# Reordering the small work around the projections of an adaLN Mamba2 block with a binarized feed-forward layer

## The chip, the cores and the metric

The kernel runs on one core of one Trainium2 chip. The metric is the device time of one execution in microseconds (us). All arithmetic is fp32. The engines are called PE (matmul), PEld (weight load of PE, overlapping it), DVE (VectorE), ACT (ScalarE), POOL (GpSimd) and SP (SyncE, which issues most of the DMAs).

## The reference

Input is x of 4 sequences of 512 tokens with 512 features, and a condition c of 4 x 512. Cut to what matters:

```
mod = (silu(c) @ wmod) split into sa, ca, ga, sb, cb, gb      # one row for each sequence
ga, gb = sign(ga)*max(|ga|, 0.25), sign(gb)*max(|gb|, 0.25)
h   = layernorm(x)*(1 + ca) + sa
x   = x + ga * mamba(h)
h   = layernorm(x)*(1 + cb) + sb
x   = x + gb * (h @ bw.T + bias)

bw = stop_gradient(where(w >= 0, 1, -1)*alpha - w) + w,   alpha = mean(|w|) by row

mamba(h):
  xBC, z, A = h @ in_proj_w.T       # 2048 + 1024 + 64 columns
  x, B, C   = silu(causal conv of xBC, 4 taps)   # x: 64 heads of 16; B, C: 8 groups of 64 states
  dt        = softplus(A)
  y         = chunked scan over chunks of 128 tokens, decay exp(-cumsum(dt)) for each head
  y         = y + D * x/dt
  return (y * silu(z + z_bias)) @ out_proj_w.T
```

The binarized weight bw takes just two values in each row, alpha and -alpha. The forward value of `(bw - w) + w` is bw up to rounding.

## The kernel before, in words

The 2048 tokens are cut into eight "halves" h of T = 256 tokens, two for each sequence. A half has two chunks c of 128 tokens, and a chunk four pairs gp of the eight groups. A triple (h, c, gp) is a unit; there are 64, eight to a half. The program is a list of steps, one for each unit (the loop at L822 to L840). In each step come, in the order in which they are written,

- the listed work of this step (`steps`): the *front* of the next half, and the *tails* of chunks that are done;
- `burst` (L593): the small products gy of C with the state for this unit, and of C with B for the unit two steps on;
- `stage2` (L630 to L696): the products py of decays and x, the sum yt, the product with z (POOL, L672), and the state's update (xd on POOL L679, pst on PE L684);
- for the unit two steps on, `stage0` (loads of the running sums into decay tiles, L536 and after) and `stage1` (16 exps on ACT, L544, eight for each of two decay tiles; the mask multiply on DVE, L622). Four decay tiles, numbered 87 to 90 in the built program, are used by turns in pairs.

The front of a half (list `FRONT`, L765 on; half 1 has `SECOND`, half 0 has `FIRST`) runs under the units of the half before. It holds the layer norm; `f_hT` (PE transposes phT, L330, of which four ACT passes make hT, L347); `f_dt` (below); the projections with causal convolution of B, C and x (`conv_pair`: products at L432, an ACT pass at L445, three DVE taps at L449, a tanh and a product); turns of B and x to tokens (pt_xt, L462); and `f_z`, four tiles z_0 to z_3 (products pp_z at L432, two ACT passes uz at L511, the tanh thz at L515, a product on DVE). Before the change the list has z_0 and z_1 at step 8, z_2 at 9 and z_3 at 10; hT and f_dt of the following half come at step 3 of its own list, which is step 11 of that of z.

`f_dt` (L353 to L406) makes the step sizes: eight products pa (L366), k from 0 to 3 and both chunks, then a chain on DVE and ACT to dt, a scan on DVE, and four DMAs to memory on SP's queue: sh to sums_d (L387), es to e_d (L391), two of r to r_d (L405). They are read back, spread over partitions, by `stage0` and `f_xt`.

The tails of a chunk are `tail1` (the output projection po, L716, the residual and the second layer norm), `tail2` (four transposes ph, L735, and ACT passes to h, L737) and `tail3` (the products pf with the binarized weight, L753). They stand at the three steps after the chunk's end, with other offsets for the last three chunks (L811 to L814); tail3 of (7, 0) is called at the end of tail1 of (7, 1).

`signs` (L267 to L279) loads 128 rows of the feed-forward weight and makes sw, ±alpha: alpha by a DVE reduction (L272) and a scaling (L273), two DVE passes (L275, L276), and on POOL the subtraction and the addition of the weight (L277, L278). `turned_signs` (L281 to L286) transposes it on PE (pbw, L285) and copies it into bwT with ACT. Both are done once, for four row blocks o, in the first half's units.

What sets the order: each engine runs its queue in the order in which the scheduler put it there. The scheduler takes the program's order as priority. Three things bend it by hand. `issue_after` holds an instruction back in that order until another one is placed. `glued` (L208 to L213) places the first of a group and then the others right behind it at a raised priority. `behind` issues a piece after the last projection of its half (`H[h]["last"]`). PSUM has five banks ("mm") taken by turns for everything but gy and py, which have a bank each.

Of the kernel before, what the change touches and what calls it, by code (L numbers as in the profile page):

```python
# [2 lines left out]

# [8 lines left out]
F32 = mybir.dt.float32  # L12
AF = mybir.ActivationFunctionType
ALU = mybir.AluOpType
AX = mybir.AxisListType
PSUM = bass.MemoryType.PSUM
P = 128

B, L, DM = 4, 512, 512
# [20 lines left out]
def adaln_mamba_block(  # L40
# [164 lines left out]
        for v in (cw, cb, zb):  # L205
            nc.vector.tensor_scalar(v, v, 0.5, None, ALU.mult)

    def glued(products):  # L208

        first = products[0]()  # L210
        with tc.issue_after(first.ins), tc.high_priority(offset=1000):
            for product in products[1:]:
                product()  # L213
# [53 lines left out]
    def signs(o):  # L267

        fw = wk.tile([P, DM], F32, tag="h2", name=f"fw{o}")
        nc.sync.dma_start(fw, ffn_w[o * P : (o + 1) * P, :])  # L270
        alpha = wk.tile([P, 1], F32, tag="rs1", name=f"alpha{o}")
        nc.vector.tensor_reduce(alpha, fw, AX.X, ALU.add, apply_absolute_value=True)  # L272
        nc.vector.tensor_scalar(alpha, alpha, 1.0 / DM, None, ALU.mult)  # L273
        sw = wk.tile([P, DM], F32, tag="CB"[o % 2], name=f"sw{o}", bufs=3)
        nc.vector.tensor_scalar(sw, fw, 0.0, 2.0, ALU.is_ge, ALU.mult)  # L275
        nc.vector.tensor_scalar(sw, sw, -1.0, alpha, ALU.add, ALU.mult)  # L276
        nc.gpsimd.tensor_sub(sw, sw, fw)  # L277
        nc.gpsimd.tensor_add(sw, sw, fw)  # L278
        sws[o] = sw  # L279

    def turned_signs(h, o):  # L281
        sw = sws.pop(o)
        pt = ps.tile([P, NK, P], F32, tag="mm", name=f"pbw{o}")
        for i in range(NK):
            nc.tensor.transpose(pt[:, i, :], sw[:, i * P : (i + 1) * P], ident)  # L285
        nc.scalar.copy(bwT[:, :, o * P : (o + 1) * P], pt)  # L286


    def layer_norm(tiles, name, into=None):
# [63 lines left out]
    def f_dt(h):  # L353

        hT = H[h]["hT"]

        def small(tag, bufs=1):  # L360
            return wk.tile([P, CH], F32, tag=tag, name=f"{tag}_{h}", bufs=bufs)

        pa = ps.tile([P, CH], F32, tag="mm", name=f"pa_{h}")
        for k in range(NK):
            for c in range(2):
                mm(pa[c * NH : (c + 1) * NH, :], win[:, k, NCONV + DI :],  # L366
                   hT[:, k, KS - 1 + c * CH : KS - 1 + (c + 1) * CH], start=(k == 0), stop=(k == NK - 1))
        u, r, q, dt, relu = (small(n) for n in ("du", "dr", "dq", "da", "dl"))
        nc.vector.tensor_scalar(relu, pa, 0.0, None, ALU.max)
        nc.scalar.activation(u, pa, AF.Abs)  # L370
        nc.scalar.activation(u, u, AF.Exp, scale=-1.0)
        nc.vector.tensor_scalar(r, u, 2.0, None, ALU.add)
        nc.vector.reciprocal(r, r)
        nc.vector.tensor_mul(u, u, r)
        nc.vector.tensor_mul(q, u, u)
        nc.vector.tensor_scalar(dt, q, SERIES[0], None, ALU.mult)
        for cf in SERIES[1:]:
            nc.vector.scalar_tensor_tensor(dt, dt, cf, q, ALU.add, ALU.mult)
        nc.vector.scalar_tensor_tensor(dt, dt, 1.0, u, ALU.add, ALU.mult)
        nc.vector.scalar_tensor_tensor(dt, dt, 2.0, relu, ALU.mult, ALU.add)  # L380

        up = relu
        nc.vector.tensor_tensor_scan(up, ones, dt, 0.0, ALU.mult, ALU.add)
        sh = small("sh", 2)
        nc.vector.tensor_scalar(sh, up, up[:, CH // 2 - 1 : CH // 2], None, ALU.subtract)
        with tc.issue_after(last_win):
            nc.sync.dma_start(sums_d[h].rearrange("c h s -> (c h) s"), sh)  # L387
        es = small("es", 2)
        nc.scalar.activation(es, up, AF.Exp, scale=-1.0)
        with tc.issue_after(last_win):  # L390
            nc.sync.dma_start(e_d[h].rearrange("c h s -> (c h) s"), es)  # L391

        ntot = wk.tile([P, 1], F32, tag="ntot", name=f"ntot_{h}", bufs=1)
        nc.vector.tensor_scalar(ntot, up[:, CH - 1 : CH], -1.0, None, ALU.mult)
        ed = u
        nc.scalar.activation(ed, up, AF.Exp, bias=ntot)

        dg = q
        nc.vector.tensor_scalar(dg, ident, es[:, CH - 1 : CH], None, ALU.mult)

        nc.vector.reciprocal(r, dt)
        nc.vector.tensor_scalar(r, r, dsk, None, ALU.mult)
        with tc.issue_after(last_win):
            for c in range(2):
                nc.sync.dma_start(r_d[h, :, c, :], r[c * NH : (c + 1) * NH, :])  # L405
        H[h].update(turn=(sh, ed, dg))  # L406

    def first_dt(h):
# [21 lines left out]
    def proj(pm, h, col, lo):  # L430
        for k in range(NK):
            last = mm(pm, win[:, k, col : col + P], H[h]["hT"][:, k, lo:], start=(k == 0), stop=(k == NK - 1))  # L432
        return last.ins

    def conv_pair(h, t0, name, dst=None):

# [156 lines left out]
    def burst(old, new):  # L593

        gy = ps.tile([P, 2, 4, CH], F32, tag="gy", bufs=1, name="gy_" + "_".join(map(str, old or new)))
        products = []
        if old is not None:
            h, c, gp = old
            k = (h % HPB) * 2 + c
            if k > 0:  # L600
                products += by_rows(gy, 1, h, c, gp, states[h // HPB, k][:, gp, :])
                G[old, 1] = gy
        if new is not None:
            h, c, gp = new
            products += by_rows(gy, 0, h, c, gp, H[h]["B"][gp // 2][:, gp % 2, c * CH : (c + 1) * CH])
            G[new, 0] = gy
        glued(products)

    def stage1(h, c, gp):

# [16 lines left out]
    def stage2(h, c, gp):  # L627
# [18 lines left out]
        for r in range(2):  # L646
            glued([
                partial(
                    mm, py[32 * j : 32 * j + 32, r, :],
                    xp[:, r * 2 * P + 32 * (2 * j + q) : r * 2 * P + 32 * (2 * j + q) + 32],  # L650
                    ets[r][:, 2 * j + q, :], start=(q == 0), stop=(q == 1),
                )
                for q in range(2) for j in range(HPG // 2)
            ])

        cs = slice(c * CH, (c + 1) * CH)
        zg = H[h]["z"][gp][:, :, cs]
# [53 lines left out]
    def tail1(h, c):  # L711
        b = h // HPB
        x2 = tails[h, c]
        po = ps.tile([P, DM], F32, tag="mm", name=f"po_{h}_{c}")
        for g in range(NKI):
            last_po = mm(po, H[h]["z"][g // 2][:, g % 2, c * CH : (c + 1) * CH], wout[:, g, :],  # L716
                         start=(g == 0), stop=(g == NKI - 1))
        t = wk.tile([P, DM], F32, tag="t", name=f"t_{h}_{c}", bufs=1)
        nc.vector.tensor_mul(t, po, gates[b][:, 0, :])
        nc.vector.tensor_add(x2, x2, t)  # L720
        layer_norm([x2], f"f{h}_{c}", [t])
        nc.gpsimd.tensor_add(x2, x2, gates[b][:, 2, :])
        tails[h, c] = (x2, t)
        if (h, c) == (NHALF - 1, 1):

            with tc.issue_after(last_po.ins):
                tail3(h, 0)

# [14 lines left out]
    def tail3(h, c):  # L743
# [5 lines left out]
        for i in range(parts):  # L749
            pf = ps.tile([P, n], F32, tag="mm", name=f"pf{i}_{h}_{c}")  # L750
            cols = slice(i * n, (i + 1) * n)
            for k in range(NK):
                mm(pf, h2[:, k, :], bwT[:, k, cols], start=(k == 0), stop=(k == NK - 1))  # L753
            o = wk.tile([P, n], F32, tag="h2", name=f"o{i}_{h}_{c}")
            nc.vector.tensor_mul(o, pf, gates[b][:, 1, cols])
            nc.vector.tensor_add(o, o, x2[:, cols])
            nc.sync.dma_start(out[h * T + c * CH : h * T + (c + 1) * CH, cols], o)

    def behind(h, f, *args):
# [7 lines left out]
        (4, f_B, (0,)), (4, f_C, (0,)), (5, f_x, (0,)), (5, f_x, (1,)), (5, behind, (f_turned_sums,)), (5, behind, (f_Bt, 0)),  # L767
        (6, f_B, (1,)), (6, behind, (f_xt, 0)), (6, f_C, (1,)), (6, behind, (f_xt, 1)),
        (7, f_x, (2,)), (7, behind, (f_Bt, 1)), (7, f_x, (3,)),
        (8, f_z, (0,)), (8, behind, (f_xt, 2)), (8, f_z, (1,)), (8, behind, (f_xt, 3)),  # L770
        (9, f_z, (2,)), (10, f_z, (3,)),
    ]

    FIRST = [
# [14 lines left out]
    NU = 2 * NP  # L789
    steps = {}  # L790

    def at(step, f, *args):
        steps.setdefault(step, []).append((f, args))

    for h in range(NHALF):
        for step, f, args in (FIRST, SECOND)[h] if h < 2 else FRONT:
            at(max(0, h - 1) * NU + step, f, h, *args)
        if h % HPB == 0:
            at(h * NU + 3, load_gates, h // HPB)
        if h == 0:  # L800
# [2 lines left out]
            at(2, load_wout)  # L803
            for o in range(NK):
                at(o // 2 + 2, signs, o)
                at(o // 2 + 4, behind, 1, turned_signs, o)
    for h in range(NHALF):
        for c in range(2):
            end = h * NU + (c + 1) * NP
            at(end - 1, load_res, h, c)  # L810

            late = {(NHALF - 1, 0): (1, 3), (NHALF - 2, 1): (0, 1, 3)}.get((h, c), (0, 1, 2))
            for tail, step in zip((tail1, tail2, tail3), late):
                at(end + step, tail, h, c)  # L814

# [6 lines left out]
    for step in range(-1, max(steps) + 1):  # L822
# [9 lines left out]
        elif step < len(units):  # L832
            if new or not is_first(*units[step][:2]):
                burst(units[step], new[0] if new else None)
            stage2(*units[step])
            for unit in POST.get(step, []):
                ahead(*unit)
            for unit in new:
# [44 lines left out]
```

## Time and profile before

| what | value |
|---|---|
| runs, us | 753.33, 754.66, 755.84 (median 754.66) |
| profiled execution, us | 755.08 |
| its span, us | 753.4 |
| mean granted TensorE clock | 0.984 |
| DMA | 99.25 MB, mean 132 GB/s |
| L544 exps on ACT | 960 instructions, 293.3 us |
| L432 products of pp_x, pp_z, pp_B | 119.7, 118.1, 62.2 us |
| L716 products of po | 256 instructions, 114.2 us |

The span runs from the first to the last instruction of the profiled execution; about 1.7 us of its time lie around it. An fp32 product appears in the trace as two passes of PE, so a group of eight products counts 16. A row of the groups reads: line, engine, operation, output<-inputs, tile sizes, count, then busy time and mean ns of one, then the engine's idle time just before, with what ended most of it. In the timeline a row is a run of like instructions; the bracket is the idle time before it. A row of waits names the engine and its line, what it waited for, the total, the number of times and the longest.

### The profile page before, as it was taken

How to read it: one execution, taken by the hardware profiler on the slowest of the kernel's cores; microseconds unless marked ns; L12 is line 12 of the kernel's file. 1: busy time of each engine (PE TensorE's matmuls, PEld its weight loads, DVE VectorE, ACT ScalarE, POOL GpSimd, SP SyncE). 2: the span in 40 equal slices, each digit the busy share in tenths (PEclk: the TensorE clock that was granted, in tenths of full speed). 3: DMA queues.
4: the chain of work that ended last, by engine and by line, in shares of the span. 5: the costliest groups of instructions: out<-in, count | busy, mean ns of one | idle time of the engine just before them, and what ended most of it. 6: DMA issues, size and time to landing. Idle time of an engine off the chain costs nothing. (4 is left out here: it accounts for less than half of the span.)

```text
span 753.4 us, 15095 instructions
## 1 busy us (share of the span) xinstructions
PE 713.0 (95%) x5196; PEld 505.6 (67%) x5196; DVE 610.8 (81%) x1226; ACT 520.1 (69%) x1503; POOL 258.5 (34%) x293
## 2 busy tenths in 40 slices
PE   6999868999999999999999999999999999999977
PEld 3786646766678666767677666786666766776643
DVE  3869888876998689976999669986898849996983
ACT  2486557749696587776777596875868758798920
POOL 4022345443143322343242341353213332334540
PEclk9999979999999999999999999999999999999989
DMA  8991583636553363424563355343634337455710
GB/s 282 313 291 42 188 193 96 166 80 144 117 142 105 84 173 105 130 68 112 142 154 105 75 142 136 113 127 90 163 89 111 93 84 182 123 161 124 161 35 28
DMA packets 121308, 99.25 MB, mean 132 GB/s; under 512 B 73984, under 2 KB 99840, under 8 KB 121232
## 3 DMA queue, kind: packets, MB, share of 16 engines
q1 hardware_dynamic: 120944, 97.76, 49.8%
q8 instruction: 41, 0.67, 0.4%
q10 hardware_dynamic: 288, 0.52, 0.2%
q14 instruction: 35, 0.29, 0.1%
HBM read 92.47 MB, written 5.79 MB: 130 GB/s over the span
## 5 line engine op out<-in xcount | busy, mean ns | idle before, releaser
L544 ACT ACTIVATE decay<-decay,st 128x128 f32<-128x128 f32 x960 | 293.3, 396 | 13.5 <-DMA decay<-sums_d 13.2
L622 DVE SCALAR_TENSOR_TENSOR decay<-decay,gm 128x1024 f32<-128x1024 f32 x120 | 155.3, 1295 | 28.3 <-ACT decay L544 26.4
L432 PE MATMUL pp_x<-hT,win 128*128 128x259 f32 x512 | 119.7, 388 | 0.0
L432 PE MATMUL pp_z<-hT,win 128*128 128x256 f32 x512 | 118.1, 383 | 0.0
L716 PE MATMUL po<-wout,z 128*128 128x512 f32 x256 | 114.2, 598 | 0.0
L679 POOL TENSOR_TENSOR xd<-xpad,st 128x256 f32<-128x256 f32 x48 | 35.0, 729 | 212.5 <-PE pst L684 161.1
L432 PEld LDWEIGHTS pp_x<-hT,win 128*128 128x128 f32 x512 | 96.2, 192 | 17.3 <-issue 2.6
L432 PEld LDWEIGHTS pp_z<-hT,win 128*128 128x128 f32 x512 | 94.3, 189 | 16.1 <-issue 3.0
L669 POOL TENSOR_TENSOR yt<-yt,xs 128x256 f32<-128x256 f32 x46 | 43.7, 950 | 128.5 <-DVE yt L668 115.9
L716 PEld LDWEIGHTS po<-wout,z 128*128 128x128 f32 x256 | 47.9, 191 | 53.8 <-issue 53.2
L449 DVE SCALAR_TENSOR_TENSOR u_x<-pp_x,cw,u_x 128x256 f32<-128x256 f32 x192 | 82.7, 474 | 0.8 <-ACT u_x L445 0.3
L213 PE MATMUL py<-decay,xpad 128*32 128x128 f32 x1680 | 68.8, 280 | 0.0
L511 ACT ACTIVATE uz<-pp_z,zb 128x256 f32<-128x256 f32 x64 | 26.8, 468 | 58.3 <-PE pp_z L432 58.3
L432 PE MATMUL pp_B<-hT,win 128*128 128x259 f32 x256 | 62.2, 395 | 0.8 <-DVE u_x L449 0.7
L672 POOL TENSOR_TENSOR z<-yt,z 128x256 f32<-128x256 f32 x62 | 57.2, 922 | 11.6 <-DVE yt L671 8.2
L502 POOL TENSOR_TENSOR xs<-u_x,rr 128x512 f32<-128x512 f32 x32 | 44.1, 1378 | 46.4 <-DVE u_x L454 38.4
L753 PE MATMUL pf<-bwT,h 128*128 128x512 f32 (+1 forms) x136 | 59.3, 576 | 0.6 <-ACT h L737 0.6
L432 PE MATMUL pp_C<-hT,win 128*128 128x259 f32 x256 | 59.5, 385 | 0.0
L445 ACT ACTIVATE u_x<-pp_x,cb,cw 128x256 f32<-128x256 f32 x64 | 35.1, 559 | 33.1 <-PE pp_x L432 32.9
L210 PE MATMUL py<-decay,xpad 128*32 128x128 f32 x240 | 48.0, 282 | 8.5 <-ACT decay L544 6.8
L432 PEld LDWEIGHTS pp_B<-hT,win 128*128 128x128 f32 x256 | 48.1, 194 | 11.2 <-DVE u_x L449 1.5
L432 PEld LDWEIGHTS pp_C<-hT,win 128*128 128x128 f32 x256 | 48.4, 192 | 7.8 <-issue 0.5
(155 smaller groups left out, 1144.5 us busy)
## 6 DMA issues: line engine op xcount, KB each, us to landing
decay<-sums_d SPq DMA_DIRECT2D x120, 256.0 KB
decay<-sums_d SPq DMA_DIRECT2D x120, 128.0 KB
rr<-r_d SPq DMA_DIRECT2D x64, 128.0 KB
e<-e_d SPq DMA_DIRECT2D x96, 64.0 KB
win<-in_w_inT SPq DMA_DIRECT2D x4, 1024.0 KB
xr<-in_x SPq DMA_DIRECT2D x16, 256.0 KB
res<-o SPq DMA_DIRECT2D x15, 256.0 KB
x<-in_x SPq DMA_DIRECT2D x14, 256.0 KB
```

What stands on the lines that cost most here:

```text
L210: first = products[0]()
L213: product()
L432: last = mm(pm, win[:, k, col : col + P], H[h]["hT"][:, k, lo:], start=(k == 0), stop=(k == NK - 1))
L445: nc.scalar.activation(u[:, j, :], pm[:, KS - 1 :], AF.Identity, bias=cb[:, t : t + 1], scale=cw[:, t, KS - 1 : KS])
L449: nc.vector.scalar_tensor_tensor(u[:, j, :], pm[:, k : k + T], cw[:, t, k : k + 1], u[:, j, :], ALU.mult, ALU.add)
L502: nc.gpsimd.tensor_tensor(xs, xc, rr, ALU.mult)
L544: nc.scalar.activation(ets[r][:, i, :], ets[r][:, i, :], AF.Exp, bias=H[h]["st"][:, hd : hd + 1], scale=-1.0)
L622: nc.vector.scalar_tensor_tensor(ets[r], ets[r], 1.0, bc_mid(gm[:, r, :], HPG), ALU.min, ALU.mult)
L669: ew.tensor_add(t, t, xs)
L672: ew.tensor_mul(zg, t, zg)
L716: last_po = mm(po, H[h]["z"][g // 2][:, g % 2, c * CH : (c + 1) * CH], wout[:, g, :], start=(g == 0), stop=(g == NKI - 1))
L753: mm(pf, h2[:, k, :], bwT[:, k, cols], start=(k == 0), stop=(k == NK - 1))
```

## The change

It has eight parts.

1. `signs` makes ±0.5 with one DVE pass and multiplies by the row's sum of |w| on ACT; the two POOL passes, the scaling of alpha and the second DVE pass are gone. The factor 2/DM is applied by ACT in the copy of `turned_signs`.
2. `turned_signs` comes one step later, and last in its steps' lists.
3. `glued` takes an instruction after which the first of the group is placed. `burst` and the py products of `stage2` give the newest projection product, so that they stand behind their step's projections on PE.
4. The eight pa products of `f_dt` are glued into one piece, and k runs from 3 down to 0 for h > 0.
5. For h > 1, `f_dt` is called after `stage2` of its step (`rear`) and no longer in the step's list.
6. The four DMAs of `f_dt` are issued from GpSimd's queue for h > 0.
7. The z tiles come at steps 8, 9, 10 and 11, and the turn of x_3 at step 9.
8. The tails: tail3 of (0, 0) comes one step later. tail2 of (7, 0) is called within tail1 of (7, 1), ahead of its last two products, and tail3 of (7, 0) as before after it; the two parts of the last o take another buffer tag.

```diff
-    def glued(products):
-        first = products[0]()
+    def glued(products, after=None):
+        with tc.issue_after(after) if after else nullcontext():
+            first = products[0]()
         with tc.issue_after(first.ins), tc.high_priority(offset=1000):
...
         nc.vector.tensor_reduce(alpha, fw, AX.X, ALU.add, apply_absolute_value=True)
-        nc.vector.tensor_scalar(alpha, alpha, 1.0 / DM, None, ALU.mult)
         sw = wk.tile([P, DM], F32, tag="CB"[o % 2], name=f"sw{o}", bufs=3)
-        nc.vector.tensor_scalar(sw, fw, 0.0, 2.0, ALU.is_ge, ALU.mult)
-        nc.vector.tensor_scalar(sw, sw, -1.0, alpha, ALU.add, ALU.mult)
-        nc.gpsimd.tensor_sub(sw, sw, fw)
-        nc.gpsimd.tensor_add(sw, sw, fw)
+        nc.vector.tensor_scalar(sw, fw, 0.0, 0.5, ALU.is_ge, ALU.subtract)
+        nc.scalar.activation(sw, sw, AF.Identity, scale=alpha)
...
-        nc.scalar.copy(bwT[:, :, o * P : (o + 1) * P], pt)
+        nc.scalar.activation(bwT[:, :, o * P : (o + 1) * P], pt, AF.Copy, scale=2.0 / DM)
...
+        queue = nc.sync if h == 0 else nc.gpsimd
...
-        for k in range(NK):
-            for c in range(2):
-                mm(pa[c * NH : (c + 1) * NH, :], win[:, k, NCONV + DI :],
-                   hT[:, k, KS - 1 + c * CH : KS - 1 + (c + 1) * CH], start=(k == 0), stop=(k == NK - 1))
+        ks = range(NK) if h == 0 else range(NK - 1, -1, -1)
+        glued([
+            partial(
+                mm, pa[c * NH : (c + 1) * NH, :], win[:, k, NCONV + DI :],
+                hT[:, k, KS - 1 + c * CH : KS - 1 + (c + 1) * CH], start=(k == ks[0]), stop=(k == ks[-1]),
+            )
+            for k in ks for c in range(2)
+        ])
...
-            nc.sync.dma_start(sums_d[h].rearrange("c h s -> (c h) s"), sh)
+            queue.dma_start(sums_d[h].rearrange("c h s -> (c h) s"), sh)
...
+        newest["proj"] = last.ins
         return last.ins
...
-        glued(products)
+        glued(products, newest["proj"])
...
+        last = (h, c) == (NHALF - 1, 1)
         for g in range(NKI):
+            if last and g == NKI - 2:
+                with tc.issue_after(last_po.ins):
+                    tail2(h, 0)
...
-        (8, f_z, (0,)), (8, behind, (f_xt, 2)), (8, f_z, (1,)), (8, behind, (f_xt, 3)),
-        (9, f_z, (2,)), (10, f_z, (3,)),
+        (8, f_z, (0,)), (8, behind, (f_xt, 2)), (9, f_z, (1,)), (9, behind, (f_xt, 3)),
+        (10, f_z, (2,)), (11, f_z, (3,)),
...
+            into = rear if f is f_dt and h > 1 else steps
+            into.setdefault(max(0, h - 1) * NU + step, []).append((f, (h, *args)))
...
-                at(o // 2 + 4, behind, 1, turned_signs, o)
+    for o in range(NK):
+        at(o // 2 + 5, behind, 1, turned_signs, o)
...
-            late = {(NHALF - 1, 0): (1, 3), (NHALF - 2, 1): (0, 1, 3)}.get((h, c), (0, 1, 2))
+            late = {(0, 0): (0, 1, 3), (NHALF - 1, 0): (2,), (NHALF - 2, 1): (0, 1, 3)}.get((h, c), (0, 1, 2))
...
             stage2(*units[step])
+            for f, args in rear.get(step, []):
+                f(*args)
```

The DMAs of es and of r change their queue in the same manner as that of sh.

More of the change, by code (lines that the diff above doesn't have):

```diff
@@ L1 @@
-from contextlib import ExitStack
+from contextlib import ExitStack, nullcontext
 from functools import partial
@@ L390, in f_dt @@
         with tc.issue_after(last_win):
-            nc.sync.dma_start(e_d[h].rearrange("c h s -> (c h) s"), es)
+            queue.dma_start(e_d[h].rearrange("c h s -> (c h) s"), es)
         ntot = wk.tile([P, 1], F32, tag="ntot", name=f"ntot_{h}", bufs=1)
@@ L404, in f_dt @@
             for c in range(2):
-                nc.sync.dma_start(r_d[h, :, c, :], r[c * NH : (c + 1) * NH, :])
+                queue.dma_start(r_d[h, :, c, :], r[c * NH : (c + 1) * NH, :])
         H[h].update(turn=(sh, ed, dg))
@@ L432, in proj @@
             last = mm(pm, win[:, k, col : col + P], H[h]["hT"][:, k, lo:], start=(k == 0), stop=(k == NK - 1))
+        newest["proj"] = last.ins
         return last.ins
+    newest = {}
     def conv_pair(h, t0, name, dst=None):
@@ L653, in stage2 @@
                 for q in range(2) for j in range(HPG // 2)
-            ])
+            ], newest["proj"])
         cs = slice(c * CH, (c + 1) * CH)
@@ L723, in tail1 @@
         tails[h, c] = (x2, t)
-        if (h, c) == (NHALF - 1, 1):
+        if last:
             with tc.issue_after(last_po.ins):
@@ L753, in tail3 @@
                 mm(pf, h2[:, k, :], bwT[:, k, cols], start=(k == 0), stop=(k == NK - 1))
-            o = wk.tile([P, n], F32, tag="h2", name=f"o{i}_{h}_{c}")
+            o = wk.tile([P, n], F32, tag="h2" if parts == 1 else "th", name=f"o{i}_{h}_{c}")
             nc.vector.tensor_mul(o, pf, gates[b][:, 1, cols])
@@ L790, in adaln_mamba_block @@
     steps = {}
+    rear = {}
     def at(step, f, *args):
@@ L796, in adaln_mamba_block @@
         for step, f, args in (FIRST, SECOND)[h] if h < 2 else FRONT:
-            at(max(0, h - 1) * NU + step, f, h, *args)
+            into = rear if f is f_dt and h > 1 else steps
+            into.setdefault(max(0, h - 1) * NU + step, []).append((f, (h, *args)))
         if h % HPB == 0:
```

## The prediction

> **What bounds the kernel now.** I began with the busy times on the page, and one stretch of the middle by windows (columns: stretch and its length, then busy time and count of PE, PEld, DVE, ACT and POOL, granted clock, DMA share, GB/s).
>
> ```profile
> PE 713.0 (95%) x5196; PEld 505.6 (67%) x5196; DVE 610.8 (81%) x1226; ACT 520.1 (69%) x1503; POOL 258.5 (34%) x293
> 300.00:350.00 50.00, 49.75 (x361) 36.59 (x354) 40.75 (x80) 34.29 (x99) 21.81 (x26) 1.00 0.42 107
> ```
>
> PE is busy 713.0 of 753.4 us, and in the middle 49.75 of 50. None of its matmuls is removed, so the change can win only PE's idle time, and the half clock that follows an idle. Where that is, the waits of PE tell (total, times, longest):
>
> ```profile
> PE pbw L285 <- DVE u_C L449: 7.2, 1, 7.2
> PE py L210 <- ACT decay L544: 6.8, 6, 2.4
> ...
> PE pa L366 <- ACT hT L347: 3.8, 4, 1.2
> PE ph L735 <- DVE t L300: 3.8, 2, 3.3
> PE ph L735 <- ACT decay L544: 2.0, 1, 2.0
> ...
> PE pbw L285 <- POOL sw L278: 1.3, 1, 1.3
> ```
>
> I looked each one up in PE's timeline (start, duration, and in brackets the idle time before it with its releaser). The largest:
>
> ```profile
> 99.48 1.09 PE L285 MATMUL pbw<-ident,sw 128*128 128x128 f32 x4 [7.21 <-DVE u_C L449]
> 101.92 1.11 PE L285 MATMUL pbw<-ident,sw 128*128 128x128 f32 x4 [1.35 <-POOL sw L278]
> ```
>
> Last I read the clock by windows. It was 0.50 in 95.60:105.80, 0.51 in 126.30:129.70 and in 566.60:570.00, and 0.50 in 729.20:733.90: always after idles of PE of 7.21, 2.02, 2.38 and 3.33 us, never after those of 1.0 to 1.5. At half clock four pst passes took 0.70 us instead of 0.44 (factor 1.59), sixteen pp_x passes 5.18 against 3.72 of the like pp_z (1.39). So a stretch of 3.4 us costs 0.96 to 1.27; I take 1.2.
>
> **What the Trainium skill says.** "TensorE: Matmul & The Clock Gate", Part 1, has the clock drop to half after an idle window of about 3.4 us and return after a busy one. The stretches here are 3.4 us or multiples of it, which agrees, but idles of 2.02 and 2.38 us sufficed. The same page, Part 2, has matmuls run strictly in program order, with only weight loads pulled ahead, and ACT and DVE first in, first out; the trace agrees: PE stood 7.21 us before pbw with pp_x behind it. "DMA: Bandwidth & Descriptors", "SWDGE vs HWDGE vs iDMA", has GpSimd write its DMAs' descriptors in software, with about 1 us to the first byte against 0.6; no GpSimd DMA is in the trace of before.
>
> **The change part by part.** I wrote out the order of instructions of the built program on each engine and laid durations of the trace along it, start to start.
>
> 1. *Signs (L270 to L286).* Eight GpSimd passes (4 x 1.492 and 4 x 1.305 = 11.2 us), four alpha scalings (4 x 0.144) and the dearer half of L276 go; four ACT passes of about 0.6 us (as thz, 128x512, 0.634) come, and turned_signs moves a step later and behind the step's projections. At most this wins 7.21 + 1.35, and of the 4.97 us that PE was busy at half clock some 1.4: 10.0. What is late next: the third and fourth pp_x get the PSUM banks that pbw waited for, and these are freed by DVE's u_C taps. DVE is busy all of 96:100 and saves only about 4 us here. Walking DVE's order I get about 4 us of wait at pp_x, so the gain is **6.0** (bounds 2 and 10).
> 2. *Products behind their step's projections.* ph that stood 2.02 us at 125.60 now runs after a projection: 2.02 + 1.2 = **3.2**. The six py waits on ACT's exps (0.85, 0.81, 2.38 and three of 0.92, 6.8 together, one with a half clock) get a projection of 1.8 to 3.7 us before them: 6.8 + 1.2 = **8.0**. The cover is that projection; without it (pp_B itself waits for banks) some 2 us come back. pp_B's three waits of 0.25 go too: **0.7**.
> 3. *Tail.* The last ph waits 3.33 us for DVE's layer norm, then 4.7 us run at half clock, which cost 1.8. With tail2 of (7,0) before the last two products of po and tail3 after, this is covered: **5.1** (bounds 2 and 5.5).
> 4. *pa (f_dt).* Its three waits of 1.16 at h = 2, 4, 6 vanish as such: **3.5**. But the new order makes larger ones. In before, z_3 came at step 10; its copies were over long before hT:
>
> ```profile
> 176.38 0.83 ACT L511 ACTIVATE uz<-pp_z,zb 128x256 f32<-128x256 f32 x2
> 177.09 2.45 ACT L544 ACTIVATE decay<-decay,st 128x128 f32<-128x128 f32 x8
> 179.43 0.65 ACT L515 ACTIVATE thz<-uz 128x512 f32<-128x512 f32 x1
> 179.95 2.46 ACT L544 ACTIVATE decay<-decay,st 128x128 f32<-128x128 f32 x8
> 182.29 1.92 ACT L347 ACTIVATE hT<-phT,modT 128x256 f32<-128x256 f32 x4
> ...
> 182.91 0.44 PE L366 MATMUL pa<-hT,win 128*64 128x128 f32 x4 [1.16 <-ACT hT L347]
> ```
>
> The reader sees that ACT's queue, not the matmul, sets when pa may start. Now z_3 is at step 11, next to phT. At h = 2, 4, 6 PE's order is pp_z_3, phT (0.97), gy (0.65), py (1.01), pst (0.37), pa: it is at pa 3.0 us after pp_z_3. ACT's order from pp_z_3's end is two uz (0.71), 8 exps (2.34), thz (0.52), three hT (1.44), 8 exps (2.34), the last hT (0.58): 8.0 us with the start. As k is reversed, pa's first product needs just that last hT. Wait: 8.0 - 3.0 = 5.0. At h = 3, 5, 7 the order is uz (0.36), 8 exps (2.34), uz (0.36), hT (0.48), thz (0.52), three hT (1.5): 5.6; PE has 2.8 (gy is smaller): 2.8. Together 3 x 5.0 + 3 x 2.8 = **23.4 lost**. All six exceed 2.02 us, so I charge a half clock each: 6 x 1.2 = **7.2 lost** (bounds 0 and 11). At h = 1, pa stands right behind phT and asks for the last hT, which I put 2.5 us later (ACT's last hT at 77.1, PE free at 74.7); PE had waited 1.07 at that place, so **1.5 lost**. The same reckoning on before (ACT's hT from 182.29, the first over at 182.75, PE free at 181.75) gives 1.0 to 1.2, as measured.
> 5. *DMAs on GpSimd's queue.* 28 issues (sums, e_d, two r, seven halves) leave SP, and with them SP's wait for es, behind which decay loads stood:
>
> ```profile
> SPq L391 <- ACT es L389: 66.4, 7, 10.4
> ```
>
> I count nothing for that: the loads are needed later than they land, but for what point 2 counts. On POOL the issues wait for es, sh and r, with xd, yt, z and rs_f queued behind; the chain from pa to es takes 13 to 16 us, and the next yt is ready only some 17 us after pa, so most of it is hidden. An issue costs between 0.3 us (SP's) and 2 us (my bound); POOL is 34% busy. I take 0, with bounds of -2 (SP's relief) and +14 (2 us in each half).
>
> Sum against the profiled execution (755.08, span 753.4 and 1.7 around it): gains 6.0 + 3.2 + 8.0 + 0.7 + 5.1 + 3.5 = 26.5; losses 23.4 + 7.2 + 1.5 = 32.1; 755.1 + 5.6 = 760.7. The median of the runs, 754.66, lies 0.4 lower: **760**.
>
> **The rivals.**
> - *No new wait at pa, faster.* One mechanism at one place: PE's arrival at pa against ACT's last hT. If exps are not in the way as I reckon, pa waits as before and the gains stand: 755 - 26.5 + 3.5 + 1.5 = 733 or so, with the wait halved 745. For it: ACT is 69% busy and stood idle before many uz (58.3 us in all). Against: the order is fixed, and uz_3 cannot start before pp_z_3 ends. It decides where the mean wait at pa, clock included, is below (26.5 - 1.5) / 6 = 4.2 us; I have 5.1.
> - *No matter.* The waits come but the clock stays full, or pbw's wait goes entirely: 760 - 7 = 753 to 756.
> - *GpSimd's queue blocks.* Where an issue waits for es, z and rs_f behind it are late, and py's bank with them: up to 2 us a half, 761 to 774. For it: no such DMA was ever measured here; against: POOL's 66% of idle.
> - *The signs' wait moves to pp_x whole.* Then 4 more, 764; it lies in the forecast's range.
>
> **How the numbers follow.** Faster rival 0.35 (0.12 of it below 735), no matter 0.12, forecast (757 to 768) 0.44, GpSimd's queue above 768 0.09. A measurement of this kernel tells about 0.3%, or 2.3 us, from no change. Faster 0.35, same 0.12, slower 0.53. Leaving out 0.12 below and 0.08 above gives 735 to 768; the likeliest case alone spans 757 to 768.
>
> **What would show it.** Right: PE's waits list pa on hT with some 23 us in six, the longest about 5, each followed by half clock; the pbw row is gone and pp_x waits about 4 us for DVE u_x or u_C; no py row for ACT's exps; the last ph has no 3 us wait. Wrong: pa's waits stay below 2 us, or ACT runs the last hT ahead of the exps; or POOL's queue shows long waits for es with PE waiting for z or yt.

## The result, and the profile after

The changed kernel takes 784.45 us (median; 783.92 to 789.10) against 754.20 of the kernel before, run alongside it: 1.0417 times as long, 95% interval 1.0378 to 1.0455. It is slower by 30.2 us, where I had forecast slower by 5.6 and a range that ended at 768. The sign was right, the size was not.

The profiled execution of the kernel after has a span of 787.4 us (789.10 us in all, the slowest of its four runs, 4.7 above their median), 34.0 more than that of before. First the busy times of the page:

```profile
PE 723.0 (92%) x5196; PEld 514.8 (65%) x5196; DVE 602.0 (76%) x1218; ACT 523.4 (66%) x1507; POOL 256.2 (33%) x313
```

PE has the same 5196 instructions, but is busy for 10.0 us more, and idle for 787.4 - 723.0 = 64.4 us instead of 40.4, 24.0 more. These two make the 34.0. The waits of PE (total, times, longest) tell the 24.0:

```profile
PE pa L211 <- ACT hT L346: 27.4, 8, 5.0
PE pg L220 <- DVE sc L196: 6.2, 1, 6.2
PE pp_x L438 <- DVE u_C L458: 6.2, 2, 5.5
PE pst L693 <- ACT xpad L497: 3.9, 1, 3.9
PE pst L693 <- DVE u_x L458: 3.4, 3, 1.4
PE ph L748 <- DVE t L299: 2.2, 5, 0.7
```

The row of pa is up from 3.8 to 27.4, 23.6 more, which alone is nearly all the added idle time. The row of pg, at the start, is the same in before. The pbw rows (8.5 together) are gone, but pp_x has 6.2; the py rows on ACT's exps (6.8) are gone, but pst has 7.3; those of ph come to 5.9 in all, as they had to 5.8. The chain of ACT and PE around pa at half 2, in the timelines (first PE, then ACT), shows the wait that the prediction worked out, 5.0 us:

```profile
188.69 3.72 PE L438 MATMUL pp_z<-hT,win 128*128 128x256 f32 x16
192.25 1.04 PE L329 MATMUL phT<-ident,x 128*128 128x128 f32 x8
...
194.87 0.44 PE L693 MATMUL pst<-xd,bt 128*64 128x128 f32 x4
200.33 0.47 PE L211 MATMUL pa<-hT,win 128*64 128x128 f32 x1 [5.02 <-ACT hT L346]
```

```profile
192.45 0.84 ACT L520 ACTIVATE uz<-pp_z,zb 128x256 f32<-128x256 f32 x2 [1.90 <-PE pp_z L438]
193.18 2.44 ACT L553 ACTIVATE decay<-decay,st 128x128 f32<-128x128 f32 x8
195.52 0.62 ACT L524 ACTIVATE thz<-uz 128x512 f32<-128x512 f32 x1
196.04 1.46 ACT L346 ACTIVATE hT<-phT,modT 128x256 f32<-128x256 f32 x3
197.38 2.44 ACT L553 ACTIVATE decay<-decay,st 128x128 f32<-128x128 f32 x8
199.72 0.56 ACT L346 ACTIVATE hT<-phT,modT 128x256 f32<-128x256 f32 x1
```

ACT is not late by its load; it had stood idle for 1.90 us before uz. It is its *order*: the last hT is behind 16 exps, made for units that come later, and pa, with k reversed, asks for that hT first.

The 10.0 us more of busy time are for the most part the clock. A table of windows of 1 us over the whole span gives the time at half clock: 23.9 us in before, 52.0 in after, of which 27.2 right behind the waits of pa at halves 2 to 6. One of them, by windows (the wait, then what follows; the first number after the counts is the clock):

```profile
195.00:200.40 5.40, 0.38 (x6) 0.14 (x8) 3.53 (x5) 5.40 (x17) 1.51 (x3) 0.96 0.87 188
200.40:203.70 3.30, 3.30 (x20) 2.75 (x21) 1.40 (x3) 2.95 (x12) 0.74 (x1) 0.55 0.60 150
```

Busy time and half-clock time move together over the kernels below that have the same products: 706.5 us + 0.29 x half-clock time meets PE's busy time of fourteen of fifteen profiled executions within 2.5 us (713.4 for 713.0 in before, 721.6 for 723.0 in after; one kernel, pa put back, lies 4.7 above, and why is not known). By this fit some 8 of the 10.0 us are the clock. So a span is read as busy time at full clock, plus idle time, plus about 0.3 of the half-clock time.

### The profile page after: what moved, and what is told of

Its sections match the earlier page's. It is cut to its first block, busy times and chain, and to the rows that moved or that the text cites. A ratio compares the mean times of both kernels' runs of the same rounds, so it can differ in the third digit from the quotient of the medians.

```text
span 787.4 us, 15135 instructions
## 1 busy us (share of the span) xinstructions
PE 723.0 (92%) x5196; PEld 514.8 (65%) x5196; DVE 602.0 (76%) x1218; ACT 523.4 (66%) x1507; POOL 256.2 (33%) x313
## 4 chain that ended last, share of the span: by engine, by line
PE 56%; ACT 14%; DVE 13%; DMA 6%; issue 6%; POOL 3%; SPq 1%; ACTq 0%; DVEq 0%; POOLq 0%
PE pp_z L438 10%; PE pp_x L438 9%; ACT decay L553 8%; PE po L730 8%; PE pf L766 6%; PE pp_B L438 5%; PE pp_C L438 5%; DMA decay<-sums_d 3%; DVE decay L631 3%; PE py L214 2%; PE py L211 2%; PE gy L211 2%; DMA fw<-in_ffn_w 2%; DVE u_x L458 1%; ACT win L553 1%
## 5 line engine op out<-in xcount | busy, mean ns | idle before, releaser
L438 PE MATMUL pp_x<-hT,win 128*128 128x259 f32 x512 | 123.7, 397 | 6.2 <-DVE u_C L458 6.2
L438 PE MATMUL pp_z<-hT,win 128*128 128x256 f32 x512 | 120.5, 388 | 0.0
L438 PEld LDWEIGHTS pp_x<-hT,win 128*128 128x128 f32 x512 | 98.3, 196 | 25.0 <-ACT decay L553 5.7
L688 POOL TENSOR_TENSOR xd<-xpad,st 128x256 f32<-128x256 f32 x48 | 38.5, 803 | 167.6 <-PE pst L693 110.1
L458 DVE SCALAR_TENSOR_TENSOR u_x<-pp_x,cw,u_x 128x256 f32<-128x256 f32 x192 | 86.6, 478 | 4.0 <-ACT u_x L454 2.1
L438 PE MATMUL pp_B<-hT,win 128*128 128x259 f32 x256 | 67.0, 418 | 1.8 <-DVE u_x L458 1.7
L214 PE MATMUL py<-decay,xpad 128*32 128x128 f32 x1680 | 65.4, 275 | 0.0
L681 POOL TENSOR_TENSOR z<-yt,z 128x256 f32<-128x256 f32 x62 | 51.6, 832 | 39.1 <-DVE z L526 18.9
L438 PEld LDWEIGHTS pp_B<-hT,win 128*128 128x128 f32 x256 | 51.8, 209 | 14.4 <-issue 2.7
L214 PEld LDWEIGHTS py<-decay,xpad 128*32 128x32 f32 x1680 | 48.1, 109 | 0.0
```

Of the source, the lines that this page charges most:

```text
L458: nc.vector.scalar_tensor_tensor(u[:, j, :], pm[:, k : k + T], cw[:, t, k : k + 1], u[:, j, :], ALU.mult, ALU.add)
L681: ew.tensor_mul(zg, t, zg)
L688: nc.gpsimd.tensor_tensor(xd, xg, by_head(H[h]["ed"][:, hd0 : hd0 + HPP]), ALU.mult)
```

## The experiments

Each difference below is that of a kernel's median from the median of the kernel before, run alongside it (754.45 to 755.31 us); ratios have their 95% interval. Distances from the kernel after are taken between two such differences, unless both times are given.

**Undo the late z.**

```diff
-        (8, f_z, (0,)), (8, behind, (f_xt, 2)), (9, f_z, (1,)), (9, behind, (f_xt, 3)),
-        (10, f_z, (2,)), (11, f_z, (3,)),
+        (8, f_z, (0,)), (8, behind, (f_xt, 2)), (8, f_z, (1,)), (8, behind, (f_xt, 3)),
+        (9, f_z, (2,)), (10, f_z, (3,)),
```

> The kernel after, with the z tiles at their old steps (8, 8, 9, 10). Theory A (the loss is made where z_3 stands right ahead of phT: ACT's queue after pp_z_3 holds the last hT back and pa waits, and the half clock after it): pa's waits on hT fall from 27.4 us to under 6, PE has no half clock there, and the time falls from 784 by 23 of idle and about 7 of clock, to 752 to 757. Theory B (the units' products behind their projections cost by themselves, in many small waits): pa's waits fall as well, but new waits of gy, py, pst and ph keep it at 763 to 772.

753.77 us, -1.5, ratio 0.9983 (0.9967 to 0.9999). The waits of PE on hT at pa fall to 2.8 us, of which 2.4 at half 1; half-clock time to 18.4. This one edit takes back 30.2 + 1.5 = 31.8 us, so the loss needs the late z. The edit moves all of z; that it is z_3 next to phT which counts, the next run shows. But it also shows that all other parts together win 1.5 us, where I had counted 23.

**Turn phT and hT ahead of z_3.**

```diff
-            into.setdefault(..., []).append((f, (h, *args)))
+            todo = into.setdefault(..., [])
+            todo.insert(0 if f is f_hT and h > 1 else len(todo), (f, (h, *args)))
```

> The kernel after, with the transposes phT and ACT's hT of halves 2 to 7 placed ahead of pp_z_3 in their step; all else as after. PE then has 3.7 us of pp_z_3 and 2 us of the unit between phT and pa. Theory A: pa's waits on hT go from 27.4 us to about 3 (that of half 1 stays at 2.5), 784 falls to 747 to 753, below the kernel before, since the other gains stay. Theory B: 760 to 768.

759.58 us, +4.3, ratio 1.0052 (1.0034 to 1.0071): 26 of the 30 are back, though z stays late; but it missed both theories' numbers. At the even halves pa's wait is gone. At the odd ones ACT's order became one hT, eight exps, three hT, as its timeline shows, and pa waited 2.19 us at 274.22:

```profile
269.90 0.57 ACT L346 ACTIVATE hT<-phT,modT 128x256 f32<-128x256 f32 x1
270.35 2.47 ACT L553 ACTIVATE decay<-decay,st 128x128 f32<-128x128 f32 x8
272.68 1.49 ACT L346 ACTIVATE hT<-phT,modT 128x256 f32<-128x256 f32 x3
```

It is the same cause in small: exps placed between the hT.

**Fill the wait with useless products, first try.** The products' output is overwritten by pa.

```diff
+        fill = 0 if h < 2 else (24, 12)[h % 2]
         glued([
+            partial(mm, pa[c * NH : (c + 1) * NH, :], win[:, 0, NCONV + DI :], ident, start=True, stop=True)
+            for i in range(fill // 2) for c in range(2)
+        ] + [
```

> The kernel after, with 24 (even halves) or 12 (odd halves) useless products in the place where PE waits for hT, written into pa's bank and then overwritten; they take 1.7 to 3.4 us of each wait. Theory A with the clock as a cost of its own: the waits for hT shrink by the products' time, the half clock after pa (27 us in all after the kernel's five pa waits) goes, and the time falls by 7 to 9 to 775 to 777. If the half clock has no price (these stretches wait for something else anyway): 783 to 785. If the products delay PE: above 786.

766.39 us, +11.1, ratio 1.0158 (1.0114 to 1.0203), 19 less than after: twice what I expected, and for a reason of its own. With the fill ahead of it, pa's first real product came later in the order than four of the products of pp_B, which ran before the last hT was there; so PE did useful work in the rest of the wait. The experiment mixed two things, and a later run, with the fill alone, repeats it cleanly.

**z and pa alone, on the kernel before** (the edits of f_dt, `rear` and the z steps from the change, nothing else).

> The kernel before, with only the parts on f_dt and z: pa's products in one piece with k from 3 down, f_dt behind its step's unit, z at steps 8, 9, 10, 11. No change to the signs, the glue's place, the queue or the tails. Theory A: nearly the whole loss is here: 754 + 24 + 7 = 780 to 787. Theory B: 754 + 24 of idle at most, and less clock, 762 to 772, as the rest of the loss belongs to the other parts.

768.29 us, +13.0, ratio 1.0156 (1.0134 to 1.0177): less than half the loss. Here pa waits 8.9 us in seven, the longest 2.2. The units' products are not bound to their step's projections, so gy and py of the next unit got between pst and pa and took part of the wait.

**pa back in its old form, z late.**

```diff
-        glued([ ... k from 3 down ... ])
+        for k in range(NK):
+            for c in range(2):
+                mm(pa[...], ...)
...
-            into = rear if f is f_dt and h > 1 else steps
+            into = steps
```

> The kernel after, with f_dt back in its step's list, pa's products not glued and k from 0 up; z stays at the late steps. Theory A1 (what costs is pa as one piece that asks for the last hT first: PE can't use the hT that are ready): pa and the first products of pp_B are laid between, the waits for hT fall from 27 us to about 10 to 14 and most of the half clock goes, 762 to 768. Theory A2 (late z alone costs, as ACT's queue sets when the last hT comes, whoever asks for it): the waits move to pp_B and the time stays at 778 to 784.

766.53 us, +12.1, ratio 1.0164 (1.0119 to 1.0209): 18 less than after. The waits for hT are 12.1 us in eight, the longest 1.9, and only one of them, that of 1.88 us at half 7, has half clock behind it (6.8 us). With pa loose, PE takes the hT as they come, and lays products of pp_B between. So more than half of the loss needs pa as one piece, too. The rest does not: against the kernel with z and pa both put back (-4.9, below), the late z with a loose pa still costs 12.1 + 4.9 = 17.0 us.

**The units' products behind the newest projection, alone on before** (the edits of `glued`, `burst` and `stage2` in the change).

> The kernel before, with only the products of the units placed behind the newest projection. The prediction's working: the waits of py and ph on ACT go, 9 us of idle with two half clocks, 11 us less: 744. Theory C (what PE does not wait for at py it waits for in the next bank or at the next user of the same exps, ACT's and DVE's chain being nearly as long): PE's idle stays within 3 us of the 40.4 of before, 752 to 757.

754.07 us, -0.4, ratio 0.9983 (0.9961 to 1.0004): nothing that can be told. The idle time is 40.5 us, against 40.4. Where it went, the waits of PE show:

```profile
PE pp_B L433 <- ACT st L426: 6.7, 3, 3.3
...
PE py L211 <- ACT decay L548: 2.8, 3, 0.9
```

Three of the six py waits on ACT's exps, those of 0.92, are still there; the other three are gone, and pp_B waits in their place. The timeline of ACT at one such place, with that of PE:

```profile
209.02 2.44 ACT L548 ACTIVATE decay<-decay,st 128x128 f32<-128x128 f32 x8
211.36 0.55 ACT L449 ACTIVATE u_x<-pp_x,cb,cw 128x256 f32<-128x256 f32 x1
211.81 0.41 ACT L426 COPY st<-pn 128x320 f32<-128x320 f32 x1
```

```profile
212.26 3.77 PE L433 MATMUL pp_B<-hT,win 128*128 128x259 f32 x16 [1.63 <-ACT st L426]
```

In before, at the same place:

```profile
213.50 0.27 PE L210 MATMUL py<-decay,xpad 128*32 128x128 f32 x1 [0.85 <-ACT decay L544]
214.21 3.77 PE L432 MATMUL pp_B<-hT,win 128*128 128x259 f32 x16
```

```profile
213.74 0.42 ACT L425 COPY st<-pn 128x320 f32<-128x320 f32 x1
```

There py waited 0.85 us for the eight exps, ran 0.7 us, and pp_B came at 214.21 with no wait, just after st (213.74 + 0.42). Now pp_B comes first and waits 1.63 for st, which stands two places behind those exps. ACT's queue sets the time of both; at this place it makes no difference which product waits first.

**The same, with st copied by DVE.**

```diff
-        nc.scalar.copy(st, pn)
+        nc.vector.tensor_copy(st, pn)
```

> The kernel before, with the products of the units behind the newest projection, and the copy of the turned sums (st from pn) made by DVE instead of ACT. Theory C (in the kernel with the first of these edits alone PE waited at pp_B for that copy, 6.7 us in three, because it stood in ACT's queue behind the same exps that py had waited for): pp_B's waits go below 2 us, PE's idle falls by 5 to 6, and the time to 746 to 750. If DVE, 80% busy, makes the copy as late as ACT did: 753 to 757.

750.34 us, -4.8, ratio 0.9943 (0.9920 to 0.9966): some 4 better than with the products alone.

```profile
PE pp_B L433 <- DVE st L426: 1.9, 3, 1.3
```

The waits of pp_B for st are 1.9 us, and a gain appears, though idle time fell by only 2.0, not the 5 to 6 expected, as waits of 1.3 at pp_B for the copy of bt and of 1.6 at pst came. That is what one would see if part of the gain lay behind one more instruction of ACT's queue. It isn't proof: the copy on DVE with the products left in their old place was not run, so what of the 4.8 us needs both edits is not known.

**The signs alone, on before** (the edits of `signs`, `turned_signs` and the step later).

> The kernel before, with only the new signs (one DVE pass, one ACT pass, no GpSimd) and turned_signs a step later. The prediction's working: 6 less, 749. Theory C: pbw's waits of 8.5 us become waits of pp_x for DVE, which itself waits for the load of fw behind the 2 MB of wout, and for banks that ACT's copies free behind its exps: 752 to 758.

755.86 us, +1.4, ratio 1.0018 (1.0005 to 1.0031). pbw's 8.5 us are gone, but two new waits have come:

```profile
PE pp_x L429 <- DVE u_C L446: 5.3, 1, 5.3
...
PE pf L750 <- ACT bwT L283: 2.2, 1, 2.2
```

py's are 1.3 longer, so that next to nothing is left of the 8.5. The wait of pf for bwT belongs to this run alone: turned_signs comes a step later here, but tail3 of (0, 0), which uses bwT, stays where it was, while the change moves both. The kernel after has no such wait. Without it the signs would win some 0.8 us (an estimate: 2.2 less than the +1.4), still far from the 6 counted. In the kernel after there is one more thing in DVE's queue, which I had not seen at all:

```profile
98.81 0.69 DVE L273 TENSOR_REDUCE alpha<-fw 128x1 f32<-128x512 f32 x1 [3.72 <-DMA fw<-in_ffn_w]
```

DVE waits 3.72 us for the load of fw, which SP issued right behind the 2 MB of wout, and the taps of u_C, on which pp_x's bank hangs, stand behind it. In the run with the signs alone DVE's wait for fw was only 0.40 us, at 107.06, after pp_x's wait; there pp_x waited 5.3 without it.

**The tails alone, on before.**

> The kernel before, with only the new places of the last tails (tail3 of (0, 0) a step later, tail2 of (7, 0) ahead of the last two products of po). The prediction's working: 3.3 us of idle and 6.8 of half clock in the tail go, 5 less: 750. Theory C: the tail's chain through DVE's layer norm stays the end, 1 to 2 less: 753 to 754.

749.72 us, -4.7, ratio 0.9942 (0.9919 to 0.9964), as predicted. The 3.3 us wait of ph is gone (0.4 is left of ph's waits for DVE's t), and 5.4 us of half clock went with it. Nothing else stood behind that wait.

**GpSimd's queue alone, on before.**

> The kernel before, with only the four DMAs of f_dt on GpSimd's queue for h over 0. The prediction's working: no change, 752 to 756. Theory Q (POOL waits 13 us for es with yt, z and rs_f behind it): 1 to 2 us lost in each of seven halves, 761 to 768. Theory Q' (SP's loads come earlier, which they had waited for): 749 to 752.

754.09 us, -1.1, ratio 0.9987 (0.9974 to 1.0000): no loss. POOL did stand still for es, as its waits show, yet PE has no wait for POOL's z or yt:

```profile
POOL e_d L393 <- ACT es L391: 76.9, 7, 12.8
```

Here too three of py's waits for exps went (6.8 to 2.8 us), and 2.5 us came back at pt_bt, pp_B and ph, behind ACT's exps and st.

**pa in one piece alone, on before, z early.**

> The kernel before, with only pa's products in one piece, k from 3 down, and f_dt behind its step's unit; z stays at the early steps. Theory A: pa's piece is harmless so long as z_3 is a step away: pa's waits on hT within 2 us of the 3.8 of before, beyond half 1 where it is 2.5; 754 to 757. Theory A1 (the piece costs by itself, as PE can't use the first hT): pa's waits at 8 to 12 and 760 to 765.

759.03 us, +3.9, ratio 1.0050 (1.0034 to 1.0066), between the two theories. The waits of pa on hT are gone but for 0.3 us, yet pbw has 9.9 in place of 8.5, py and gy 5.8 more, and pst 2.6 that it had not. Of the 4.6 us by which PE's idle time grew, 1.6 lie before 130 us, in half 1's front, and some 3 come later, in like places every second half: instead of the waits at pa, gy and py wait for DVE's masks and sums, and pst for ACT's st.

**All that loses, put together on before: z late, pa in one piece, products behind projections.**

> The kernel before, with the products of the units behind the newest projection, pa in one piece behind its step's unit, and z at the late steps; no change to signs, queue and tails. The late z and pa's piece alone cost 13.0, the products' place alone nothing, and all parts together 30.2. Theory I (these parts need each other: with the unit's products bound behind pp_z_3, nothing but phT, gy, py and pst can stand between pp_z_3 and pa): pa's waits at 24 us or more, 778 to 786. Theory J (the rest comes from the signs or from GpSimd's queue): 766 to 770.

787.51 us, +32.2, ratio 1.0414 (1.0375 to 1.0453), the loss of the whole change without its signs, its queue and its tails. The waits of PE:

```profile
PE pa L211 <- ACT hT L348: 27.5, 8, 5.0
```

So the three parts need each other for the whole loss: z_3 next to phT makes the last hT late, the bound products leave nothing to put in between, and the one piece keeps PE from using the first hT.

**Fill only, with the order kept.** The fill as above, with (40, 24) products, and every projection of a half held behind its pa.

> The kernel after, with useless products ahead of pa for halves 2 to 7: 40 (even halves, some 4.5 us) and 24 (odd halves, 2.7 us), written into pa's bank and then overwritten, and every projection of a half held behind its pa, so that the order of all other products is that of after. What PE waits for stays where it was; only the clock can change. If the half clock costs 0.36 of its length (as span = 704 + idle + 0.36 x half-clock time fits the kernels so far) and filling avoids some 27 us of it: 9 to 11 less than after, 773 to 776. If the half clock costs nothing, as PE waits there anyway: 783 to 786.

775.00 us, +19.7, ratio 1.0244 (1.0204 to 1.0285), 9.4 less than the 784.45 of after, as expected (10.5 less, when each is set against the kernel before that ran alongside). PE's timeline at half 2:

```profile
188.38 4.42 PE L214 MATMUL pa<-ident,win 128*64 128x128 f32 x77
193.46 1.09 PE L214 MATMUL pa<-hT,win 128*64 128x128 f32 x16 [0.66 <-ACT hT L346]
```

The hT come no earlier: the last one starts 7.31 us after the end of pp_z_3, here as in the kernel after. PE's order of all other products is that of after up to the last 53 us, where four products of the tails changed places. PE does 192 useless products more, and the kernel is faster, because no half clock follows any pa. Of the 30.2 us, about 10 are the clock behind these waits.

**z and pa both back**, so that signs, products' place, queue and tails are left of the change.

> The kernel after, with z at the old steps, and pa unglued, k from 0 up, f_dt in its step's list: what is left is the signs, the products' place, GpSimd's queue and the tails. One by one these gave +1.4, -0.4, -1.1 and -4.7. If they add: 754.7 - 4.8 = 750, and 3 to 4 below the same kernel with pa's piece (753.8). If they hinder one another: 753 to 757.

750.44 us, -4.9, ratio 0.9936 (0.9910 to 0.9961). One by one they gave +1.4 - 0.4 - 1.1 - 4.7 = -4.8: within the noise they add up.

**The best version that the runs point to:** the kernel before with the tails' places, the products behind projections, and st copied by DVE.

> The kernel before, with the tails' new places, the units' products behind the newest projection, and st copied by DVE. If the pieces add up: 4.9 of the tails and 4 to 8 of the other two: 742 to 746. If the copy on DVE is late: 749 to 752.

744.08 us, -11.1, ratio 0.9857 (0.9836 to 0.9878). It beats both kernels. 4.7 and 4.8 would be 9.5; the half-clock time is 6.8 us, as with z and pa both back, and less than in all others.

```profile
PE 707.8 (95%) x5196; PEld 501.8 (68%) x5196; DVE 607.7 (82%) x1234; ACT 516.8 (70%) x1495; POOL 254.1 (34%) x293
```

## Why the prediction was wrong

| step of the prediction | predicted, us | measured, us | by |
|---|---|---|---|
| 1 signs | -6.0 | +1.4 | signs alone |
| 2 products behind projections | -11.9 | -0.4 (no change) | these alone |
| 3 tail | -5.1 | -4.7 | tails alone |
| 4 pa, z, hT and clock, less the old 3.5 | +28.6 | +35.2 | 31.8 (z undone) + 3.4 (pa's piece: 753.77 - 750.44, relative to before) |
| 5 queue | 0 | -1.1 (barely a change) | queue alone |
| all | +5.6 | +30.2 (the rows add to 30.4) | the kernel after |

The failed steps are 1 and 2, the signs and the products behind their projections: of 24.6 us of error, 18.9 are theirs (7.4 and 11.5). The prediction took an idle time that has a name in PE's waits as time that comes free with the wait. It even named the danger, "without it (pp_B itself waits for banks) some 2 us come back", and priced it at nothing. In the trace of before, pp_B at 214.21 followed the end of st by 0.05 us; such a near miss says that the next wait is already there. In the run with the products alone pp_B's waits rose from 0.7 to 7.4 us, and PE's idle time was what it had been, 40.5 us. With st moved to DVE as well 4.8 us were won, less than half of the 11.9; how much of that needs both edits stays open. For the signs the next wait, pp_x on DVE's taps, was foreseen with 4 us; alone it was 5.3, and 3.5 more at pf and py, which the prediction put at nothing, ate the rest. In the kernel after pp_x waited 6.2, and before it DVE waited 3.7 for fw, a load that the walk on DVE's order had left out.

Step 4 was right in mechanism and nearly in size. The six waits were predicted as 5.0 and 2.8 and measured as 5.02, 3.45, 5.02, 3.04, 5.03 and 3.05, together 24.6 against 23.4; that of half 1 as 2.5, measured 2.45. The clock was charged with 1.2 for each of six waits, 7.2; the clean fill gives 9.4, as three of the waits had two stretches of 3.4 us with them and not one, and the sixth none. The rest, some 3, fits what pa's piece costs with z early (3.4 and 3.9 us in two kernels), which I had not counted. That the sign came right hung on this step alone: gains of 26.5 stood against losses of 32.1, and had the loss been counted a fifth smaller, the forecast would have been a gain.

The faster rival, that pa would not wait anew, was decided against where it said it would be: its point was a mean wait of 4.2 us, clock included, and (24.6 + 9.4) / 6 = 5.7. The rival of no matter fell with the clock. GpSimd's queue did not block: POOL waited 92.4 us for es in the kernel after, 76.9 in the run with the queue alone, and PE's one wait for POOL, 0.4 us for z at po, is in the run with the tails alone as well. Of what was to show the forecast right, pa's row came as written, but half clock followed five of its six waits, and pp_x's row came with 6.2 in place of about 4; "no py row for ACT's exps" came true as well, and yet proved nothing, since pst and others had rows instead.

One page of the Trainium skill bore on this. "TensorE: Matmul & The Clock Gate", Part 1, has the clock fall after an idle window of about 3.4 us; the stretches were of 3.4 and 6.8 us, but a wait of 3.04 brought one on as well, while 3.05 at half 7 did not (in the run of the three parts together, 3.03 at the same place did). From one kernel the prediction had read that 2.02 us brought it on and 1.0 to 1.5 did not. With pa put back, 6.8 us followed a wait of 1.88, and with pa's piece alone 3.4 us began at 79.18, right behind waits of 1.07 and 1.14. The same Part 1 has ACT take its instructions strictly first in, first out, and the trace agrees: the last hT stands behind eight exps while PE waits 5.02 us for it. That order is what made the last hT late.

What stays open: what the copy of st on DVE gives alone; why the next unit's products wait for DVE and ACT when pa is one piece; why the late z with a loose pa still costs 17.0 us; and when an idle of 1 to 3 us brings half clock on. The changed kernel had some at 36.09 us, behind a wait of 1.90 at pt_xt, and at 15.62, with only 0.33 just ahead.

## What to carry to other kernels

A wait in the list of a nearly full engine was worth here only the distance to the next instruction that the same releasing queue held up; look for what starts within a few tenths of a microsecond of its own releaser right after the wait. Before an operation is placed close behind its producer, count what the engine between them has queued in that span: here 16 exps of 0.3 us stood between a matmul and its 0.5 us copy, on an engine that was 66% busy. Freedom in the order (a group not glued, k from the side that is ready first) is what let PE use such a span. And bindings don't add: the products' place alone cost nothing, pa's piece alone 3.9 us, pa's piece with late z 13.0, and all three 32.2.

## What the runs showed of the hardware

Work that nobody needs can make the kernel faster: 192 useless products put into PE's waits took 9.4 us off (784.45 to 775.00), with the order of the others as it was but for four products in the tail. PE's busy time over fourteen of fifteen kernels followed 706.5 us + 0.29 x half-clock time within 2.5 us; by this estimate a wait of 5 us with 6.8 us of half clock behind it costs about 7. The length of a wait alone did not tell whether half clock came: at half 7, 3.05 us had none and, in another kernel, 3.03 us had 3.4 us of it.
